# A four-layer network on one core: fp32 turns as TensorE transposes, no longer as matmuls with the identity

## The chip, the core and the metric

The kernel runs on one core of a Trainium2 chip. The core has five engines with a queue each: TensorE (PE in the profile, with its weight loads shown apart as PEld), VectorE (DVE), ScalarE (ACT), GpSimd (POOL) and SyncE (SP), which here issues all the DMA transfers. The metric is the device time of one execution in microseconds. A profile of one execution stands beside it; its span runs from the first to the last instruction.

## What is computed

An image batch x of shape (4, 96, 64, 64) in fp32 passes through four layers. Seen as tokens it is 16,384 tokens (4 images of 4,096) of 96 channels.

- Layer 0: two Mamba blocks. Each normalises every token over its 96 channels, projects, runs a short causal convolution and a selective scan along the tokens, gates and projects back; then comes a fusion with a pooled branch and a batch norm.
- Layer 1: a 7 x 7 depthwise convolution, a norm over the channels, an MLP with a Gelu, scaling and the residual.
- Layer 2: a norm, linear attention without a softmax, and an MLP in emulated fp8.
- Layer 3: a norm, a filter in Fourier space along the tokens, and another MLP in emulated fp8.

The parts that the change touches, cut from the reference:

```python
# layer 0, in each of its two blocks
mu = seq.mean(-1, keepdims=True)
var = ((seq - mu) ** 2).mean(-1, keepdims=True)
h = (seq - mu) * jax.lax.rsqrt(var + EPS) * ln_g + ln_b
...
# layer 1
h = conv_general_dilated(x, conv_w, padding=((3, 3), (3, 3)), feature_group_count=dim)
h = jnp.transpose(h + conv_b[None, :, None, None], (0, 2, 3, 1))
h = (h - mu) * jax.lax.rsqrt(var + LN_EPS) * ln_g + ln_b
h = jax.nn.gelu(jnp.einsum('bhwc,cf->bhwf', h, w1) + b1, approximate=False)
h = jnp.einsum('bhwf,fc->bhwc', h, w2) + b2
...
# layer 2
attn = jnp.einsum('bhnd,bhmd->bhnm', q, k) * D ** (-0.5)
y = jnp.einsum('bhnm,bhmd->bhnd', attn, v)
```

## The kernel before

Channels lie on the partitions (96 of them) and tokens along the free dimension nearly everywhere. In four places the kernel needs tokens on the partitions, or comes back from there, and turns tiles of 128 tokens by 96 or 97 channels. A matmul computes the transpose of its stationary operand times the moving one, so a product of a tile with the identity turns it. The result lands in PSUM and ACT or DVE copies it out.

- Layer 0, `first_stage`, slot -3 (L308). The work is cut into 32 items: 4 images by 4 chunks of 1,024 tokens by 2 blocks. Each item passes 24 scan tiles of 128 x 1,024: per tile ACT does an exponential (`da`, `dap`), PE repeats B over the partitions (`rep`, L454), DVE multiplies (L486) and scans (L490), POOL multiplies by C (L496), PE sums into `y` (L515). Beside the scans of one item run the norm and the projections of a later one, spread over time slots written by hand. In the norm `nt` holds tokens on partitions; 8 products with `ident` turn it back into `ps`, and ACT copies it into `n` (L323), which feeds the projections `w_x` and `w_z` (L210).
- Layer 1, token stage (`tokens`, `turn`, L744). For each of 16 chunks of 1,024 tokens, two loads (`o`, `xr`), an ACT scaling (L736) and a DVE addition (L737) make `t`; `turn` then turns 8 tiles into `xt_ps` in two halves of four. ACT copies the first half into `xt` (L750), DVE the second (L748).
- Layer 1, convolution: 24 groups of 4 channels, each a product of `xt` with a band matrix (1 MB a group, three buffers, L761) on PE. Ahead of group 8 `consts2` prepares the constants of all later layers: its loads, its DVE and ACT work, and three small products on PE stand in the queues at that place.
- Layer 1, norm and MLP: 32 blocks of 512 tokens. `stats` (DVE, L810, L811), `roots` (ACT), `back` (DVE makes four slices `n`, L824; PE turns them into `tp_ps`, L829; DVE copies to `xc`, L831), `hidden` (PE, L838, ACT Gelu, L839) and `out` (PE, L844, DVE adds into `t`, L847).
- Layer 2, attention: 32 blocks of 512 tokens. `scale` (`v_ps`, L894, then two ACT operations), `center` (`xc_ps`, L888, then ACT's square), `norm` (DVE, L900), `turn` (PE turns 4 tiles of 128 tokens by 97 rows into `ht_ps`, L935; ACT copies to `ht`, L939), `products` (`gram`, L947), and from a lag of 11 blocks on `out` (`o_ps`, L985). The attention runs without a softmax, so the 97 x 97 product `gram` of an image is all it needs of the turned tokens. In one step of the loop `back` comes before `out`, `center` before `products`, and `turn` before `out`.

The order of the instructions on PE, DVE, ACT and POOL is the program's own, since these four are named in the manual schedule:

```python
engines = {mybir.EngineType.PE, mybir.EngineType.DVE, mybir.EngineType.Activation, mybir.EngineType.Pool}
```

SP is not among them. The order of the DMA issues on its queue is made by a scheduler, from its own estimate of when each instruction becomes ready. A load that finds its buffer still in use, or the semaphore that it would reuse still owed by an earlier load, holds back everything behind it on SP. In `consts2` the buffers `w1raw` and `w2raw` are single, so the loads for the second fp8 MLP (`f3`) wait for the casts of the first (`f2`).

The layer 1 block loop, which sets the order around L829:

```python
hidden(i)
...
for i2 in (1, 2) if i == 0 else (i + 2,):
    if i2 < 4 * n:
        back(i2)
...
if d:
    out(i - 1)
```

Of the kernel before, what the change touches and what calls it, by code (L numbers as in the profile page):

```python
# [18 lines left out]
B, C, HW, L = 4, 96, 64, 4096  # L19
# [31 lines left out]
class Net:  # L51
# [43 lines left out]
    def layer0(self, dram, scratch):  # L95
        tc, nc, ins = self.tc, self.nc, self.ins
        x_in = ins["x"]
        with ExitStack() as ctx:
# [43 lines left out]
            n = cp.tile([C + 1, T + 3], F32, name="n")  # L142
# [56 lines left out]
            def tile_ps(rows=C):  # L199
                return psum.tile([128, MB], F32, name="ps", tag="ps")[:rows]  # L200
# [54 lines left out]
            def first_stage(k):  # L255

                b, s, i = items[k]
                m = made[k]
                steps = {}

                def at_slot(t):
                    def keep(f):
                        steps.setdefault(t - 24, []).append(f)

                    return keep

                @at_slot(-11)
                def _():
                    m["xn"] = load_x(b, s, i) if k else x0
# [34 lines left out]
                @at_slot(-3)  # L304
                def _():
                    m["ps"] = [tile_ps(), tile_ps()]
                    for q in range(8):
                        nc.tensor.matmul(  # L308
                            m["ps"][q // 4][:, q % 4 * 128 : q % 4 * 128 + 128],
                            m["nt"][:, q],  # L310
                            self.ident,
                            start=True,
                            stop=True,
                        )

                @at_slot(-2)
# [251 lines left out]
            with tc.manual_schedule(engines=engines):  # L568
                gp = global_pool()
                first = min(stages[0])  # L570
                for m in range(first, last + 19):
                    k, t = divmod(m, NTL)
# [39 lines left out]
            d = cp.tile([C, 1], F32, name="bn_d0")  # L612
# [100 lines left out]
    def layer1(self, scratch, t):  # L713
        tc, nc, ins = self.tc, self.nc, self.ins
# [3 lines left out]
        with ExitStack() as ctx:  # L718
# [4 lines left out]
            with (  # L723
                tc.manual_schedule(engines=engines),
                tc.tile_pool(name="l1a", bufs=1) as wk,
                tc.tile_pool(name="l1ap", bufs=1, space=PSUM) as psum,
            ):
                for at in (slice(0, 2), slice(NR + 2, NR + 4)):
                    nc.gpsimd.memset(xt[:, :, :, at], 0.0)
                def tokens(b, s):  # L730
                    at = slice(b * L + s * T, b * L + (s + 1) * T)
                    o = wk.tile([C, T], F32, name="o", tag="o", bufs=3)
                    nc.sync.dma_start(o, scratch[:, at])
                    xr = wk.tile([C, T], F32, name="xr", tag="xr", bufs=3)
                    nc.sync.dma_start(xr, ins["x"][b, :, s * T : (s + 1) * T])
                    nc.scalar.activation(o, o, AF.Identity, scale=self.osc, bias=self.osh)  # L736
                    nc.vector.tensor_add(t[:, at], o, xr)  # L737

                def turn(b, s):
                    for h in range(2):  # L740
                        ps = psum.tile([128, 4, 128], F32, name="xt_ps", tag="xt", bufs=4)
                        for d in range(4):
                            a = b * L + s * T + (4 * h + d) * 128
                            nc.tensor.matmul(ps[:, d], t[:, a : a + 128], self.ident[:C], start=True, stop=True)  # L744
                        r = 2 + s * (T // 128) + 4 * h
                        dst = xt[:, :, b, r : r + 4].rearrange("p c r -> p r c")
                        if h:
                            nc.vector.tensor_copy(dst, ps[:, :, :C])  # L748
                        else:
                            nc.scalar.copy(dst, ps[:, :, :C])  # L750

                chunks = [(b, s) for b in range(B) for s in range(NSC)]
                tokens(*chunks[0])
                for k, chunk in enumerate(chunks):
                    if k + 1 < len(chunks):
                        tokens(*chunks[k + 1])
                    turn(*chunk)

                def load(g):
                    w = wk.tile([128, GC, 4, 128], F32, name="band", tag="band", bufs=3)  # L760
                    nc.sync.dma_start(w, ins["band"][g])  # L761
                    return w

                def outer(g):

                    x2 = wk.tile([128, 2 * GC, B, NR], F32, name="x2", tag="x2", bufs=3)
                    at = slice(g * 2 * GC, (g + 1) * 2 * GC)
                    nc.gpsimd.tensor_copy(x2[:64], xt[:64, at, :, 4:])
                    nc.gpsimd.tensor_copy(x2[64:], xt[64:, at, :, :NR])
                    return x2  # L770

                def small(rows, cols):
                    ps = psum.tile([128, 4, 128], F32, name="w_ps", tag="xt", bufs=4)
                    return ps.rearrange("p a c -> p (a c)")[:rows, :cols]

                x2 = [outer(0)]
                for g in range(C // GC):
                    if g == 8:
                        self.consts2(wk, small)
                    if g % 2 == 0 and g + 2 < C // GC:  # L780
                        x2.append(outer(g // 2 + 1))
                    w = load(g)
                    ps = psum.tile([128, GC, B, NR], F32, name="cv_ps", tag="cv", bufs=4)
                    for d in range(GC):
                        c = g * GC + d
                        for k, j in enumerate((1, 0, 2)):
                            nc.tensor.matmul(
                                ps[:, d], w[:, d, j], xt[:, c, :, 1 + j : 1 + j + NR], start=k == 0, stop=False
                            )
                        nc.tensor.matmul(ps[:, d], w[:, d, 3], x2[g // 2][:, g % 2 * GC + d], start=False, stop=True)  # L790
                    for d in range(GC):
                        c = g * GC + d
                        dst = xt[:, c, :, 2 : 2 + NR]
                        if g % 2:
                            nc.vector.tensor_scalar_add(dst, ps[:, d], cb[:, c : c + 1])
                        else:
                            nc.scalar.activation(dst, ps[:, d], AF.Identity, bias=cb[:, c : c + 1])
# [20 lines left out]
            def back(i):  # L818
                k, d = divmod(i, 4)
                n = wk.tile([128, 4, C], F32, name="n", tag="n", bufs=3)  # L820
                for q in range(4):
                    b, r = divmod(4 * i + q, NR)
                    at = slice(4 * d + q, 4 * d + q + 1)
                    nc.vector.tensor_scalar(  # L824
                        n[:, q], xt[:, :, b, 2 + r], mv[k][:, at, 0], rs[k][:, at], ALU.subtract, ALU.mult
                    )
                ps = psum.tile([C, 4, 128], F32, name="tp_ps", tag="tp", bufs=2)
                for q in range(4):
                    nc.tensor.matmul(ps[:, q], n[:, q], self.ident, start=True, stop=True)  # L829
                xc[i] = wk.tile([C, MB], F32, name="xc", tag="xc", bufs=7)  # L830
                nc.vector.tensor_copy(xc[i], ps.rearrange("p r n -> p (r n)"))  # L831

# [17 lines left out]
            n = NT // MB // 4  # L850
# [55 lines left out]
    def layer2(self, t, h3):  # L906
        tc, nc = self.tc, self.nc
        NB = L // MB
        n = B * NB
        engines = {mybir.EngineType.PE, mybir.EngineType.DVE, mybir.EngineType.Activation, mybir.EngineType.Pool}  # L910
        with ExitStack() as ctx:
# [9 lines left out]
            for k in range(2):  # L921
                h = wk.tile([C + 1, L], F32, name=f"h{k}")
# [4 lines left out]
            def block(i):  # L927
                b, s = divmod(i, NB)
                return hs[b % 2][:, s * MB : (s + 1) * MB]

            def turn(i):
                h = block(i)
                ps = psum.tile([128, 4, C + 1], F32, name="ht_ps", tag="ht")
                for d in range(4):
                    nc.tensor.matmul(  # L935
                        ps[:, d], h[:, d * 128 : (d + 1) * 128], self.ident[: C + 1, : C + 1], start=True, stop=True
                    )
                ht[i] = wk.tile([128, 4, C + 1], F32, name="ht", tag="hts", bufs=2)
                nc.scalar.copy(ht[i], ps)  # L939

# [52 lines left out]
            for j in range(2 * n + NB + 2):  # L993
# [19 lines left out]
                if 0 <= j - 3 < n:  # L1013
                    turn(j - 3)
# [473 lines left out]
```

## Time and profile before

| | us |
|---|---|
| device time, median of 3 runs | 3931.25 |
| lowest and highest run | 3930.65, 3931.9 |
| span of the profiled execution | 3923.7 |

The stages of the profiled execution, by the window view (busy us of each engine in the stretch; the bounds are rounded, since stages overlap a little at their ends):

| stretch, us | what runs | PE | DVE | ACT | POOL | PE clock |
|---|---|---|---|---|---|---|
| 0 to 25 | first loads, first norm | 18.7 | 9.2 | 7.4 | 0.8 | 1.00 |
| 2450 to 2590 | layer 0, the last items | 94.0 | 135.8 | 65.8 | 136.3 | 0.70 |
| 2590 to 2660 | end of layer 0, layer 1's token stage | 44.7 | 35.7 | 36.0 | 4.8 | 0.85 |
| 2660 to 2790 | layer 1's convolution | 91.2 | 28.7 | 18.8 | 24.8 | 0.86 |
| 3140 to 3260 | layer 2's fp8 MLP | 108.4 | 104.4 | 97.9 | 75.8 | 1.00 |
| 3330 to 3760 | layer 3's Fourier filter | 387.1 | 212.8 | 257.3 | 196.5 | 0.98 |

The page gives PE 14,174 matmuls and 14,174 weight loads. The four lines of the turns in the trace, where each fp32 product shows as two matmuls and two loads:

| line | where | matmuls | median ns of a matmul | median ns of a load | first to last start, us |
|---|---|---|---|---|---|
| L308 | layer 0's norm | 512 | 421 | 283 | 16.7 to 2430.6 |
| L744 | layer 1's token stage | 256 | 275 | 192 | 2612.2 to 2658.6 |
| L829 | layer 1's norm | 256 | 273 | 163 | 2788.8 to 2982.1 |
| L935 | layer 2's attention | 256 | 275 | 192 | 3008.3 to 3134.7 |

How to read it: matmuls are pipelined, so that the duration of one record (from its start to its modelled end) is longer than the time for which it holds PE. That time is read from one start to the next. The PE clock is the mean that was granted in the stretch, 1.00 being full speed.

### The profile page before, as it was taken

The numbers are of one execution on the slowest core, as the hardware profiler recorded it, in microseconds if no ns is written. First come the engines' busy times: TensorE is split into PE (matmuls) and PEld (weight loads), VectorE is DVE, ScalarE is ACT, GpSimd is POOL, SyncE is SP. The second block draws the span as 40 slices with busy tenths as digits, with TensorE's granted clock in tenths as the row PEclk, the third lists the DMA queues.
The fourth block names the chain that finished last, engine by engine and source line by source line (L and its number), as shares of the span: only waits on it lengthen the run. The fifth ranks groups of instructions, "written<-read, shape, count | busy, mean of one in ns | idle before, by whom it ended". The sixth has DMA issues, their size and how long they took to land. (4 is left out here: it accounts for less than half of the span.)

```text
span 3923.7 us, 45255 instructions
## 1 busy us (share of the span) xinstructions
PE 3245.2 (83%) x14174; PEld 1384.0 (35%) x14174; DVE 3158.5 (80%) x2772; ACT 2419.1 (62%) x4644; POOL 2911.1 (74%) x1443
## 2 busy tenths in 40 slices
PE   7788878887787788888878888666899988899988
PEld 3222222222222222222222222136545634666653
DVE  5999999999999999999999999962563385444649
ACT  4666667766766676667766666541345576656558
POOL 2999999999999999999999999942001054444427
PEclk8878888888889888878897888678899999999999
DMA  7567656665666566656775666646200000011102
GB/s 188 139 158 171 151 139 166 165 161 143 162 164 163 138 167 164 163 138 165 167 162 137 166 165 163 146 125 218 73 1 1 1 1 6 14 33 36 39 7 59
DMA packets 179833, 463.39 MB, mean 118 GB/s; under 512 B 52852, under 2 KB 54782, under 8 KB 176256
## 3 DMA queue, kind: packets, MB, share of 16 engines
q1 hardware_dynamic: 179592, 460.49, 47.4%
q8 instruction: 113, 1.85, 0.2%
q14 instruction: 128, 1.05, 0.1%
HBM read 386.81 MB, written 73.50 MB: 117 GB/s over the span
## 5 line engine op out<-in xcount | busy, mean ns | idle before, releaser
L496 POOL TENSOR_TENSOR hs<-hs,crep 128x1024 f32<-128x1024 f32 x768 | 1795.5, 2361 | 28.3 <-DVE hs L490 24.5
L454 PE MATMUL rep<-dbl,sel_b 32*128 32x512 f32 x1152 | 407.2, 783 | 468.4 <-DVE hs L490 436.5
L474 POOL TENSOR_TENSOR up<-udb,brep 128x1024 f32<-128x1024 f32 x256 | 604.2, 2360 | 8.5 <-DMA brep<-cd 8.5
L468 ACT ACTIVATE da<-ddb,nega 128x1024 f32<-128x1024 f32 x512 | 585.0, 1150 | 16.0 <-DVE hs L490 9.2
L468 ACT ACTIVATE dap<-ddb,nega 128x1024 f32<-128x1024 f32 x256 | 286.2, 1118 | 422.7 <-DVE hs L490 421.2
L515 PE MATMUL y<-hs,sel_r 128*32 128x512 f32 x3072 | 480.5, 693 | 5.5 <-POOL hs L496 5.4
L490 DVE TENSOR_TENSOR_SCAN hs<-da,state,rep 128x1024 f32<-128x1024 f32 x192 | 450.8, 2348 | 16.7
L490 DVE TENSOR_TENSOR_SCAN hs<-da,state,u 128x1024 f32<-128x1024 f32 x192 | 450.9, 2348 | 11.2 <-DVE u L486 1.4
L490 DVE TENSOR_TENSOR_SCAN hs<-dap,state,up 128x1024 f32<-128x1024 f32 x192 | 447.0, 2328 | 6.0 <-ACT dap L468 5.9
L454 PEld LDWEIGHTS rep<-dbl,sel_b 32*128 32x128 f32 x1152 | 108.7, 217 | 765.9 <-issue 515.6
L210 PE MATMUL ps<-n,w_x 97*64 97x512 f32 x1536 | 364.9, 617 | 8.0 <-ACT n L323 4.4
L486 DVE TENSOR_TENSOR u<-udb,rep 128x1024 f32<-128x1024 f32 x256 | 314.7, 1229 | 44.3 <-PE rep L454 13.6
L486 DVE TENSOR_TENSOR rep<-udb,rep 128x1024 f32<-128x1024 f32 x256 | 310.6, 1213 | 0.3
L1046 POOL CAST hq<-y 128x1536 fp8e5<-128x1536 f16 x64 | 93.9, 1467 | 233.5 <-issue 137.6
L210 PEld LDWEIGHTS ps<-n,w_x 97*64 97x64 f32 x1536 | 108.9, 140 | 256.6 <-issue 212.4
L515 PEld LDWEIGHTS y<-hs,sel_r 128*32 128x32 f32 x3072 | 66.3, 116 | 354.9 <-issue 187.5
L382 POOL TENSOR_TENSOR du<-delta,xc 128x512 f32<-128x512 f32 x96 | 122.2, 1273 | 64.7 <-ACT delta L366 50.4
L918 POOL MEMSET h<- 1x4096 f32 x1 | 3.5, 3506 | 223.3 <-DVE n L824 223.3
L358 ACT COPY dbl<-ps 102x512 f32<-102x512 f32 x64 | 34.4, 589 | 199.9 <-PE ps L224 199.9
L1185 POOL TENSOR_TENSOR av<-av,ec 128x780 f32<-128x780 f32 x32 | 58.8, 1836 | 132.7 <-ACT av L1182 132.7
L224 PE MATMUL ps<-xc,xproj 64*102 64x512 f32 x384 | 154.2, 963 | 3.5 <-ACT xc L344 3.5
L490 DVE TENSOR_TENSOR_SCAN hs<-da,rep 128x1024 f32<-128x1024 f32 x64 | 146.5, 2289 | 5.4
(262 smaller groups left out, 6420.4 us busy)
## 6 DMA issues: line engine op xcount, KB each, us to landing
ddb<-dd SPq DMA_DIRECT2D x768, 128.0 KB
udb<-ud SPq DMA_DIRECT2D x768, 128.0 KB
crep<-cd SPq DMA_DIRECT2D x512, 128.0 KB
brep<-cd SPq DMA_DIRECT2D x256, 128.0 KB
dd<-delta SPq DMA_DIRECT2D x64, 384.0 KB
ud<-du SPq DMA_DIRECT2D x192, 128.0 KB
band<-in_band SPq DMA_DIRECT2D x24, 1024.0 KB
x<-in_x SPq DMA_DIRECT2D x32, 384.0 KB
```

What stands on the lines that cost most here:

```text
L210: nc.tensor.matmul(ps[rows], w[:, 64 * p : 64 * p + 64], rhs[:, at.start + shift : at.stop + shift], start=k == 0, stop=k == len(ws) - 1, ...
L224: nc.tensor.matmul(ps, w[rows, p], x[rows, p], start=start and p == 0, stop=p == 2)
L382: nc.gpsimd.tensor_mul(u, m["delta"][:, of], m["xc"][:, of])
L454: nc.tensor.matmul(x[:, at], sel_b[rows, order[t][1]], made[k]["dbl"][rows, at], start=True, stop=True)
L468: nc.scalar.activation(da, made[k]["dd", h, j], AF.Exp, scale=nega[:, col : col + 1])
L474: nc.gpsimd.tensor_mul(u, made[k]["ud", h, j], made[k]["brep", g])
L486: nc.vector.tensor_mul(u, made[k]["ud", h, j], x)
L490: nc.vector.tensor_tensor_scan(hs[:, 1:], made[k].pop(("da", t)), u, 0.0 if s == 0 else st, ALU.mult, ALU.add)
L496: nc.gpsimd.tensor_mul(hs[:, :T], hs[:, 1:], made[k]["crep", order[t][1]])
L515: nc.tensor.matmul(made[k]["y", p][row : row + 32], sel_r, made[k]["hs", t][:, at], start=False, stop=True, skip_group_check=True,)
L1046: nc.gpsimd.tensor_copy(q, y2, saturate=False)
L1185: nc.gpsimd.tensor_add(v[:, 2:4], v[:, 0:2], ec)
```

## The change

In the four places `nc.tensor.matmul(out, tile, identity, start=True, stop=True)` becomes `nc.tensor.transpose(out, tile, identity)`, which is TensorE's own transpose: a matmul instruction with its transpose flag set, with the same operands. The number of turns (640) stays. In layer 1's token stage the output and the identity are also cut from 128 to 96 columns, since a transposed tile of 96 channels has 96 columns. Tiles, buffers, copies and the order written by hand on PE, DVE, ACT and POOL stay as they are. The other products with the identity (the residual of layer 0's `project`, L533) stay matmuls.

```diff
@@ -305,12 +305,8 @@
                     m["ps"] = [tile_ps(), tile_ps()]
                     for q in range(8):
-                        nc.tensor.matmul(
-                            m["ps"][q // 4][:, q % 4 * 128 : q % 4 * 128 + 128],
-                            m["nt"][:, q],
-                            self.ident,
-                            start=True,
-                            stop=True,
+                        nc.tensor.transpose(
+                            m["ps"][q // 4][:, q % 4 * 128 : q % 4 * 128 + 128], m["nt"][:, q], self.ident
                         )
@@ -741,7 +737,7 @@
                             a = b * L + s * T + (4 * h + d) * 128
-                            nc.tensor.matmul(ps[:, d], t[:, a : a + 128], self.ident[:C], start=True, stop=True)
+                            nc.tensor.transpose(ps[:, d, :C], t[:, a : a + 128], self.ident[:C, :C])
@@ -826,7 +822,7 @@
                 for q in range(4):
-                    nc.tensor.matmul(ps[:, q], n[:, q], self.ident, start=True, stop=True)
+                    nc.tensor.transpose(ps[:, q], n[:, q], self.ident)
@@ -932,9 +928,7 @@
                 for d in range(4):
-                    nc.tensor.matmul(
-                        ps[:, d], h[:, d * 128 : (d + 1) * 128], self.ident[: C + 1, : C + 1], start=True, stop=True
-                    )
+                    nc.tensor.transpose(ps[:, d], h[:, d * 128 : (d + 1) * 128], self.ident[: C + 1, : C + 1])
```

## The prediction

> **What bounds the kernel now.** I read the page's slices first, then the busy time by stage, then the waits of the longest stage, then the order in time inside the stages where the changed instructions run.
>
> ```profile
> 25.00:2450.00 2425.00, 1966.49 (x8256) 618.02 (x8252) 2320.14 (x1327) 1608.73 (x2980) 2350.88 (x1066) 0.84 0.66 159
> ...
> 2790.00:2990.00 200.00, 191.78 (x619) 93.99 (x619) 120.90 (x409) 85.56 (x121) 3.51 (x1) 0.97 0.00 1
> ...
> 3010.00:3140.00 130.00, 126.31 (x701) 80.00 (x700) 35.10 (x54) 75.07 (x141) 0.00 (x0) 1.00 0.00 1
> ```
>
> The columns are stretch, length, then busy us of PE, PEld, DVE, ACT and POOL, PE clock, DMA share and GB/s. In layer 0 (first row) DVE and POOL are busy 96% and 97%; PE, at 81%, is not the bound. In layer 1's norm and MLP (second) and in layer 2's attention (third) PE is busy 96% and 97% and nothing else exceeds 60%. So 256 of the 640 transposes lie where PE has room, 128 (L744) in the token stage paced by loads (DMA share 1.04 in 2610 to 2650), and only the 256 of L829 and L935 where PE is the bound. What each engine waited for in layer 0, 100 to 2400 us:
>
> ```profile
> DVE u L486 <- PE rep L454: 12.3, 12, 2.9
> ...
> POOL hs L496 <- DVE hs L490: 18.8, 24, 2.4
> ```
>
> DVE waited 12.3 us for PE in 2,300 us. ACT waits 60.8 us for L308 in all (44 times), but ACT is busy only 66% and loses its time again waiting for DVE's scans. Layer 1's MLP, in order of time:
>
> ```profile
> 2852.53 2.74 PE L838 MATMUL g_ps<-xc,c_w 96*128 96x512 f32 x6
> ...
> 2855.11 1.04 PE L829 MATMUL tp_ps<-ident,n 128*96 128x128 f32 x8
> ...
> 2855.98 2.74 PE L838 MATMUL g_ps<-xc,c_w 96*128 96x512 f32 x6
> ...
> 2858.50 1.14 DVE L824 TENSOR_SCALAR n<-xt,mv,rs 128x96 f32<-128x96 f32 x4
> ...
> 2858.97 1.19 PE L829 MATMUL tp_ps<-ident,n 128*96 128x128 f32 x8 [0.25 <-DVE n L824]
> ```
>
> Four transposes hold PE from 2855.11 to the next matmul at 2855.98, 0.87 to 0.88 us: 8 matmul/load pairs (each fp32 product is two) of 110 ns. The last row is different: there PE waits for DVE's `n` slices, 0.29 us each. And layer 2:
>
> ```profile
> 3129.80 1.06 PE L935 MATMUL ht_ps<-ident,h 97*128 97x97 f32 x8
> ...
> 3130.70 1.02 PE L985 MATMUL o_ps<-h,g 97*96 97x512 f32 x2
> ...
> 3131.56 1.02 PE L894 MATMUL v_ps<-sq,ones 96*96 96x512 f32 x2
> ...
> 3132.42 1.02 PE L888 MATMUL xc_ps<-t,center 96*96 96x512 f32 x2
> ...
> 3133.28 0.85 PE L947 MATMUL gram<-ht 128*97 128x97 f32 x8
> ...
> 3133.96 1.06 PE L935 MATMUL ht_ps<-ident,h 97*128 97x97 f32 x8
> ```
>
> One block takes 4.16 us of PE without a gap; four transposes hold it for 3130.70 - 3129.80 = 0.90, some 0.86 after the overlap at the start: 107 ns a pair.
>
> [...] at L935 the matmul has 97 columns, the load 128, and the pair takes 107 ns, so the load sets the pace; at `gram` (97 and 97) it is 0.68/8 = 85. [...] no row of before shows a transpose. [...] the trace has two pairs, with 430 ns for 512 columns each.
>
> **The change, part by part.** The program built from the changed kernel has 13,534 matmuls and as many loads, against 14,174: a transpose is one pair where the product was two. My estimate of a pair: [...] 80 ns at L829 (96 columns), 107 at L935 and L744 (128). Bounds: [...] one load costing what the two did, 160 and 213 ns, no gain at L935. Dearer than the old product is the rival below.
>
> *L829, 32 groups of four.* A group goes from 0.88 to 4 x 0.08 = 0.32: 0.56 off. Counted in the timeline: 27 groups from 2821.8 on, of which 5 (2834.29, 2858.97, 2883.64, 2908.30, 2932.96) wait for `n`. In those, DVE goes from one group's end through xc (0.2 + 0.61), statistics (1.69), four `n` (1.16) to the next in about 4.0 us, which no PE speed changes: 0.1 each. For the other 22, DVE's longest round is m_ps (2.58 us after the transposes), 0.2, t 0.72, `n` 1.16, and about 0.3 to the last transpose, 5.0 us, against PE's new 2.58 + 2.58 + 0.32 = 5.48: PE stays the bound. 22 x 0.56 = 12.3, plus 0.5, plus 2 for the five early groups (two at half clock, 1.99 us of records each, about 0.85; the others partly behind `n`). Sum 14.8; bounds 6 and 17.5.
>
> *L935, 32 groups.* 0.86 becomes 4 x 0.107 = 0.43. In the last 20 blocks (4.16 us, with the o_ps product) all of it counts: 8.6. In the first 10 the block takes 3.30 us, and there a second loop lies just below: ahead of the first transposes (3000.50, 3003.51, 3006.53) v_ps comes every 3.01 us, PE waiting 1.06 us for ACT's square of the last block. So those gain 0.29: 2.9. Two blocks with the small matmuls of the weights: 0.8. Sum 12.3; bounds 0 and 16.9.
>
> *L744, 16 chunks of eight.* Loads pace the chunks (about 3 us; eight transposes take 1.75). Only the last chunk's second half stands before the convolution: 8 x 0.107 instead of 1.75, so the convolution starts about 0.9 us earlier. If that were lost again, nothing.
>
> *The SP queue, which the diff does not show.* Its DMA order is not written by hand, and with the other transposes it comes out differently in the convolution. The loads of bands 3 to 7 move up among c_w1, c_w2, ls_row, wkv, wqt and wff; the last three are now issued after band 7, between it and bn1_rows, some 0.43 us each, +1.3 us. At g = 8 PE stands still for 25 us, and this is why:
>
> ```profile
> 2681.70 3.43 SPq L680 DMA_DIRECT2D bn_rows<-in_bn_rows  x1
> ...
> 2704.11 0.45 ACT L682 ACTIVATE bn_s<-bn_rows,eps 97x192 f32<-97x192 f32 x1 [15.40 <-DMA bn_rows<-in_bn_rows]
> ...
> 2711.59 0.36 DVE L664 CAST f3w1q<-w1raw 96x384 fp8e5<-96x384 f32 x1 [16.51 <-DMA w1raw<-in_f_w]
> ```
>
> bn_rows takes 22 us to land and only then does SP issue the second w1raw and w2raw, which take 7.4 us more beside a band of 1 MB. In the new order w1raw goes earlier, w2raw still waits for bn_rows, and band 9 moves behind both (the first being 0). So: -0.9 from the early start, +1.3 from the three loads, -0.36 for a cast done ahead. I take zero for the token stage and convolution together; -5 if w2raw lands before the bands, +4 if band 9 is late.
>
> *L308, layer 0.* 8 of some 75 us of work per item; hidden under DVE and POOL in steady state. In the first item PE does L308 from 16.66 to 19.4 at half clock and the convolution could start when DVE has w_x, at 18.70: 0.65 us, and the same kind of time once more before the scans run full: 1.5 in all. Bounds +3 (PE, less busy, gets a lower clock than its 0.84, and `rep` comes later) and -4.
>
> Sum: 14.8 + 12.3 + 1.5 + 0 = 28.6 us off the span of 3923.7: 3895.1. The time outside the span (3931.25 - 3923.7 = 7.5 us) stays, so 3902.6, taken as 3903.
>
> **Rivals.** *All at a quarter:* [...] 17.5 + 16.9 + 1.5 = 36 off, 3895; with the kind ends of layer 0 and the loads 3887. [...] against: in the trace loads follow columns only. *One load as dear as two:* 6 + 0 + 1.5 off, 3924, up to 3929 with the unkind ends.[...] *Slower:* [...] Place: the same 22 and 32 groups. 4 x 0.275 = 1.10 instead of 0.88 and 0.86: 22 x 0.22 + 32 x 0.24 + 0.5 = +13, 3944. It decides from 215 ns a transpose on. [...] against: 275 ns is also what the trace records for a plain 128-column matmul here (273 median at L829), pipelined at 110, so it looks like latency.
>
> **How the numbers follow.** Forecast 0.58, all at a quarter 0.16, one dear load 0.12, slower 0.14. 0.2% is 7.9 us, about what a measurement of this kernel tells from no change, so faster means below 3923.4: 0.58 + 0.16 + half of 0.12 = 0.80; same the other half and a little, 0.07; slower 0.13. The range runs over the first three cases with their ends, 3887 to 3929, and leaves the slower case out.
>
> **What would show it.** L829's groups should hold PE 0.3 to 0.45 us, L935's 0.43, with matmul counts 512, 256, 256, 256 halved. Layer 2's block should be 3.7 us, and 3.0 early on with PE waiting for `sq`. The gated groups of layer 1 should keep their 4.0 us. PE's halt at g = 8 should end within some us of 2716. A time above 3931 with pairs over 0.2 us means the slower rival; a clock under 0.97 in these two stages would be a cause I have not priced.

## The result, and the profile after

Before and after were run together, eight times each.

| | before | after |
|---|---|---|
| median, us | 3931.97 | 3919.55 |
| lowest and highest, us | 3930.65 to 3936.74 | 3900.96 to 3925.66 |
| ratio of the times, with its 95% interval | | 0.9961 (0.9947 to 0.9976) |

The change gains 12.4 us where 28.6 were forecast. The runs of after spread over 24.7 us, those of before over 6.1. The profiled execution of after is its slowest run: span 3923.9 us, no shorter than the 3923.7 of before. So the two profiles side by side show gains and losses of equal size. Read from the starts and ends of the same instructions in both:

| stretch | before, us | after, us | difference |
|---|---|---|---|
| layer 0, first scan to end of last scan | 2515.0 | 2535.2 | +20.2 |
| first turn of the token stage to first turn of L829 (L825 after): token stage, convolution | 176.6 | 180.2 | +3.6 |
| layer 1's norm and MLP, first turn to last `m_ps` | 209.0 | 198.0 | -11.0 |
| layer 2's attention, first `xc_ps` to last `ht_ps` | 136.3 | 121.4 | -14.9 |
| from there to the end | 788.7 | 790.7 | +2.0 |

The remaining +0.3 us lies in the joints between these stretches. Since the edit is shorter than what it replaces, the same lines have smaller numbers in after: L829 is L825 there, L935 is L931, L454 is L450 and L486 is L482. Layer 1's MLP in the timeline of after (start, duration, engine, line, operation; x4 means that four instructions are merged into the row):

```profile
2868.51 0.60 PE L825 MATMUL tp_ps<-ident,n 128*96 128x128 f32 x4
2868.95 5.31 PE L840 MATMUL m_ps<-g,c_w 128*96 128x512 f32 x12
...
2876.67 0.60 PE L825 MATMUL tp_ps<-ident,n 128*96 128x128 f32 x4
2877.11 2.74 PE L834 MATMUL g_ps<-xc,c_w 96*128 96x512 f32 x6
```

Four transposes are now four instructions instead of eight, and hold PE from 2876.67 to 2877.11: 0.44 us, 110 ns each. Before it was 0.88. Layer 2's attention, in the timeline of after:

```profile
3118.31 0.50 PE L931 MATMUL ht_ps<-ident,h 97*128 97x97 f32 x4
3118.64 1.02 PE L979 MATMUL o_ps<-h,g 97*96 97x512 f32 x2
3119.50 1.02 PE L890 MATMUL v_ps<-sq,ones 96*96 96x512 f32 x2
3120.37 1.02 PE L884 MATMUL xc_ps<-t,center 96*96 96x512 f32 x2
3121.22 0.85 PE L941 MATMUL gram<-ht 128*97 128x97 f32 x8
3121.91 0.50 PE L931 MATMUL ht_ps<-ident,h 97*128 97x97 f32 x4
```

The turns hold PE for 0.33 us (3118.31 to 3118.64), 83 ns each, and the block goes round in 3.60 us instead of 4.16. So the two stages where PE is the bound gained 25.9 us together, near the 27.1 that were forecast. The loss is in layer 0. What its DVE waited for from 100 to 2400 us, in the wait view of after (engine, tile, line, releaser: us in total, times, longest):

```profile
DVE u L482 <- PE rep L450: 43.4, 36, 2.9
DVE hs L486 <- ACT dap L464: 1.8, 4, 0.6
```

DVE, the bound of this stage together with POOL, waits 43.4 us for `rep` from PE, where it was 12.3, although PE has less to do. Its clock tells why. The window view of after at one of the places where the projections `w_x` follow the turns (stretch, length, busy us of PE, PEld, DVE, ACT, POOL, then PE clock, DMA share, GB/s):

```profile
1097.80:1101.90 4.10, 0.06 (x4) 0.00 (x0) 3.94 (x3) 2.40 (x6) 4.10 (x3) 0.80 0.85 229
1101.90:1111.00 9.10, 9.05 (x24) 2.40 (x28) 8.79 (x5) 2.36 (x4) 9.10 (x5) 0.53 1.02 228
```

The same view of before, at the like place of the same item:

```profile
1095.60:1098.10 2.50, 0.10 (x4) 0.03 (x1) 2.36 (x3) 2.47 (x9) 2.50 (x3) 1.00 1.04 270
1098.10:1107.90 9.80, 9.29 (x44) 2.60 (x45) 9.50 (x6) 3.47 (x8) 9.18 (x4) 1.00 1.05 232
```

After the turns PE stands idle for 4.1 us in after, 2.5 in before; then it works at a granted clock of 0.53 in after, of 1.00 in before. PE's timeline of after at that place, with idle time and its releaser in brackets:

```profile
1095.79 1.08 PE L308 MATMUL ps<-ident,nt 128*96 128x128 f32 x8
1096.80 1.06 PE L511 MATMUL y<-hs,sel_r 128*32 128x512 f32 x8
1101.95 2.08 PE L450 MATMUL rep<-dbl,sel_b 32*128 32x512 f32 x4 [4.09 <-DVE u L482]
1103.96 6.89 PE L210 MATMUL ps<-n,w_x 97*64 97x512 f32 x16
1110.79 1.06 PE L511 MATMUL y<-hs,sel_r 128*32 128x512 f32 x8
1111.78 3.66 PE L210 MATMUL ps<-n,w_x 97*64 97x512 f32 x16
1115.37 1.13 PE L450 MATMUL rep<-dbl,sel_b 32*128 32x512 f32 x4
```

And that of before:

```profile
1092.66 2.04 PE L308 MATMUL ps<-ident,nt 128*96 128x128 f32 x16 [0.68 <-ACT nt L302]
1094.63 1.06 PE L515 MATMUL y<-hs,sel_r 128*32 128x512 f32 x8
1098.10 1.13 PE L454 MATMUL rep<-dbl,sel_b 32*128 32x512 f32 x4 [2.41 <-DVE u L486]
1099.16 3.65 PE L210 MATMUL ps<-n,w_x 97*64 97x512 f32 x16
1102.75 1.06 PE L515 MATMUL y<-hs,sel_r 128*32 128x512 f32 x8
1103.74 3.65 PE L210 MATMUL ps<-n,w_x 97*64 97x512 f32 x16
1107.90 1.13 PE L454 MATMUL rep<-dbl,sel_b 32*128 32x512 f32 x4 [0.51 <-DVE hs L490]
```

The turns took 1.0 us instead of 2.0. Then the first 16 matmuls of `w_x` take 6.89 us in place of 3.65. From one `rep` to the next it is 1115.37 - 1101.95 = 13.4 us instead of 9.8. In before PE had 0.51 us to spare ahead of the second `rep`; in after it has none, and DVE waits (its timeline):

```profile
1116.54 1.23 DVE L482 TENSOR_TENSOR u<-udb,rep 128x1024 f32<-128x1024 f32 x1 [2.69 <-PE rep L450]
```

This comes back: from the first scan of one item to that of the next, before mostly takes 78.4 to 78.6 us in its steady state, while after goes round in a cycle of four items, 78.1 to 78.5, 79.1 to 79.5, 81.3 and 78.6. The place shown is the worst of the four. From the first start of the first 16 matmuls of `w_x` to the last, the mean clock from 1000 us on is 0.60, 0.50, 1.00 and 0.64 in turn in after, cycle for cycle, and 1.00 in every item of before.

The traces of before and after hold records of the granted clock, 258 and 260 of them. Each is 0.5 or 1.0, and each but the last of a trace lasts a multiple of 3.413 us. Cut into steps of this length at the bounds of the records, with PE's busy share of each step worked out from the starts of its instructions (an instruction holds PE until its end or the next start, whichever comes first), the place above reads:

```
before   step from     1090.2  1093.6  1097.0  1100.5  1103.9  1107.3
         busy share      0.80    0.61    0.69    1.00    1.00    0.85
         clock           1.0     1.0     1.0     1.0     1.0     1.0
after    step from     1090.0  1093.5  1096.9  1100.3  1103.7  1107.1  1110.5
         busy share      0.45    0.63    0.29    0.51    1.00    1.00    1.00
         clock           1.0     1.0     1.0     0.5     0.5     0.5     1.0
```

After the step with 0.29 the clock falls, and here PE fills two whole steps before it is back. By then the projections are nearly done. In the traces of before and after together the clock rose 257 times, each time after a step at least 0.84 busy, and fell 259 times, never after a step over 0.69.

Four items of the cycle take 317.4 us in after; four items of before, at 78.48 us, take 313.9. Why it is a cycle of four was not shown.

### The profile page after: what moved, and what is told of

Same layout as the page of the kernel before. It is cut to its first block, busy times and chain, and to the rows that moved or that the text cites. A ratio compares the mean times of both kernels' runs of the same rounds, so it can differ in the third digit from the quotient of the medians.

```text
span 3923.9 us, 43975 instructions
## 1 busy us (share of the span) xinstructions
PE 3205.9 (82%) x13534; PEld 1294.8 (33%) x13534; DVE 3154.4 (80%) x2772; ACT 2420.6 (62%) x4644; POOL 2911.4 (74%) x1443
## 5 line engine op out<-in xcount | busy, mean ns | idle before, releaser
L450 PE MATMUL rep<-dbl,sel_b 32*128 32x512 f32 x1152 | 407.8, 785 | 495.8 <-DVE hs L486 428.3
L486 DVE TENSOR_TENSOR_SCAN hs<-da,state,rep 128x1024 f32<-128x1024 f32 x192 | 450.8, 2348 | 16.7
L486 DVE TENSOR_TENSOR_SCAN hs<-da,state,u 128x1024 f32<-128x1024 f32 x192 | 450.9, 2348 | 11.2 <-DVE u L482 1.4
L486 DVE TENSOR_TENSOR_SCAN hs<-dap,state,up 128x1024 f32<-128x1024 f32 x192 | 446.7, 2326 | 0.4 <-ACT dap L464 0.4
L210 PE MATMUL ps<-n,w_x 97*64 97x512 f32 x1536 | 408.0, 679 | 9.3 <-ACT n L319 6.6
L482 DVE TENSOR_TENSOR u<-udb,rep 128x1024 f32<-128x1024 f32 x256 | 314.7, 1229 | 74.4 <-PE rep L450 46.0
L450 PEld LDWEIGHTS rep<-dbl,sel_b 32*128 32x128 f32 x1152 | 107.0, 214 | 794.5 <-issue 595.7
L482 DVE TENSOR_TENSOR rep<-udb,rep 128x1024 f32<-128x1024 f32 x256 | 310.3, 1212 | 0.2
L210 PEld LDWEIGHTS ps<-n,w_x 97*64 97x64 f32 x1536 | 118.6, 153 | 295.2 <-issue 243.5
L486 DVE TENSOR_TENSOR_SCAN hs<-da,rep 128x1024 f32<-128x1024 f32 x64 | 146.5, 2289 | 5.4
L486 DVE TENSOR_TENSOR_SCAN hs<-da,u 128x1024 f32<-128x1024 f32 x64 | 146.4, 2288 | 3.7 <-DVE u L482 0.5
```

The source lines that it names most:

```text
L210: nc.tensor.matmul(ps[rows], w[:, 64 * p : 64 * p + 64], rhs[:, at.start + shift : at.stop + shift], start=k == 0, stop=k == len(ws) - 1, ...
L450: nc.tensor.matmul(x[:, at], sel_b[rows, order[t][1]], made[k]["dbl"][rows, at], start=True, stop=True)
L482: nc.vector.tensor_mul(u, made[k]["ud", h, j], x)
L486: nc.vector.tensor_tensor_scan(hs[:, 1:], made[k].pop(("da", t)), u, 0.0 if s == 0 else st, ALU.mult, ALU.add)
```

## The experiments

Each kernel was timed in five rounds beside the kernel before (e4_fill has four times on record, e7_delay six). Those of layer 0 and its turns alone or undone (e1 to e4) ran together, with before at 3932.12 us; e5 to e8 together, with before at 3930.91; e9 and e10 together, with before at 3930.31. Each group ran on another chip. Between these groups the ratios are compared, not the times.

**Only layer 0's turns undone: e1_rest.** The diff is against after.

```diff
-                        nc.tensor.transpose(
-                            m["ps"][q // 4][:, q % 4 * 128 : q % 4 * 128 + 128], m["nt"][:, q], self.ident
+                        nc.tensor.matmul(
+                            m["ps"][q // 4][:, q % 4 * 128 : q % 4 * 128 + 128],
+                            m["nt"][:, q],
+                            self.ident,
+                            start=True,
+                            stop=True,
                         )
```

> The turns of layer 1 and of the attention stay transposes, layer 0's norm goes back to the matmul with the identity. Theory (the loss sits in layer 0: shorter turns there leave PE's clock low when the projections start, so that rep comes late for DVE): layer 0 goes back to about 2515 us from the first scan to the end of the last, DVE's waits for rep to about 12 us, and the median to 3902 to 3908 with a spread of a few us. Rival (the loss is not bound to these eight transposes but to the whole program's timing, or to the chip of that run): layer 0 stays near 2535 us, the median near 3920, with a spread of some 25 us.

Measured: 3903.12 us, ratio 0.9924 (0.9910 to 0.9938). Layer 0 takes 2514.9 us again, and DVE's wait reads:

```profile
DVE u L486 <- PE rep L454: 15.8, 17, 3.0
```

**Only layer 0's turns changed: e2_l0only**, the reverse: before, with the L308 block of after.

> Only layer 0's norm uses the transpose. Theory: layer 0 alone becomes 5 to 25 us longer, so the median is 3937 to 3957, slower than before, with the wide spread of the changed kernel. Rival: the turns of layer 0 are hidden either way, and the median is within 0.2% of before.

Measured: 3951.53 us, ratio 1.0042 (1.0028 to 1.0055), slower than before. Layer 0 takes 2534.6 us.

```profile
DVE u L482 <- PE rep L450: 45.0, 42, 2.8
```

The two parts nearly add up: -29.0 and +19.4 us make -9.6, against -12.4 for the whole change. Three of the four edits gain what the whole was forecast to; the fourth, priced at -1.5, gives more than half of it back.

**Each turn of layer 0 done twice: e3_twice.** The diff is against after. The second round writes the same values to the same place.

```diff
-                    for q in range(8):
+                    for q in range(16):
+                        q %= 8
                         nc.tensor.transpose(
```

> The changed kernel, with each of layer 0's eight transposes done twice, so that they hold PE as long as the eight fp32 products did (16 pairs). Theory A (the clock follows how long PE is busy, with whatever): layer 0 goes back to about 2515 us and the median to 3902 to 3908, although PE has more to do. Theory B (work in transpose mode does not count for the clock): the clock after the turns stays low, layer 0 stays at 2530 us or more, the median at 3918 or more.

Measured: 3902.11 us, ratio 0.9924 (0.9911 to 0.9936), layer 0 2513.3 us.

```profile
DVE u L483 <- PE rep L451: 11.8, 12, 2.8
```

More work on PE than in after, and layer 0 is 21.9 us shorter. What was lost is not a price of the transpose as such. It comes from the work that PE no longer does.

**Four plain fp32 products ahead of the eight transposes: e4_fill.** Again against after; the transposes overwrite the results.

```diff
+                    for q in range(4):
+                        nc.tensor.matmul(
+                            m["ps"][q // 4][:, q % 4 * 128 : q % 4 * 128 + 128],
+                            m["nt"][:, q],
+                            self.ident,
+                            start=True,
+                            stop=True,
+                        )
                     for q in range(8):
                         nc.tensor.transpose(
```

> The changed kernel, with four fp32 products ahead of layer 0's eight transposes, written to the same PSUM and overwritten by them: 8 product pairs and 8 transpose pairs, the same 16 pairs as before the change. Theory A (how long PE is busy): layer 0 about 2515 us, median 3902 to 3908. Theory B (transposes don't count): half of the old counted work, so a layer 0 between, 2515 to 2535 us. If the lost time has nothing to do with the clock, the added 0.9 us of PE work per item leaves layer 0 at 2535 us or makes it longer.

Measured: 3897.89 us, ratio 0.9915 (0.9902 to 0.9929), layer 0 2516.3 us, 15.3 us of waits for `rep`. With products as filling layer 0 comes back to 2516.3 us, with transposes to 2513.3.

**How much filling it takes: e9_half and e10_thrice.** As e3_twice, with `range(12)` and `range(24)`.

> All turns as transposes, four of L308's eight done twice (12 in place of 8 in the changed kernel and 16 in the run with each done twice). Theory (the work that PE does ahead of the projections decides its clock there): in part back, layer 0 between 2516 and 2530 us, median between 3904 and 3916, waits of u for rep between 15 and 40 us. Rival (there is one sharp limit, or the doubled work matters only by something that comes with all eight): at one of the two ends, 2513 to 2516 or 2531 to 2536.

> All turns as transposes, L308's eight done three times each (24). Theory (once the clock is up, more work ahead of the projections brings nothing more and, being off the path of VectorE, costs little): layer 0 2512 to 2517 us, median 3899 to 3905. Rival (more work goes on lifting the clock and takes away the last 12 us of waits for rep): layer 0 2503 to 2511, median 3889 to 3898. Second rival (the longer turns are late themselves): layer 0 2520 or more.

Measured with 12: 3903.65 us, ratio 0.9933 (0.9920 to 0.9945), layer 0 2516.4 us, 13.7 us of waits for `rep`: all of the loss is back with half of the doubling. Layer 0 lies at the edge of both ranges (the theory's began at 2516, the rival's ended there), but the waits and the median lie outside the theory's. So the expectation of a partial recovery failed, and what came is one of the rival's two ends: layer 0 lies 20.2 us above before with 8 turns and 1.4 with 12. With 24: 3895.83 us, 0.9917 (0.9903 to 0.9930), layer 0 2512.0 us and 10.1 us of waits, as the theory said for layer 0; the median lies in the rival's range, but the interval of its ratio and that of e3_twice overlap for the most part. PE's timeline of e9_half shows how the clock returns:

```profile
1168.18 2.08 PE L451 MATMUL rep<-dbl,sel_b 32*128 32x512 f32 x4 [4.17 <-DVE hs L487]
1170.19 2.79 PE L309 MATMUL ps<-ident,nt 128*96 128x128 f32 x12
1172.91 1.89 PE L512 MATMUL y<-hs,sel_r 128*32 128x512 f32 x8
1175.40 1.13 PE L451 MATMUL rep<-dbl,sel_b 32*128 32x512 f32 x4 [0.61 <-DVE u L483]
1176.46 3.66 PE L210 MATMUL ps<-n,w_x 97*64 97x512 f32 x16
```

and after, at the like place of an earlier item, how it does not:

```profile
1015.29 2.08 PE L450 MATMUL rep<-dbl,sel_b 32*128 32x512 f32 x4 [4.16 <-DVE hs L486]
1017.30 1.94 PE L308 MATMUL ps<-ident,nt 128*96 128x128 f32 x8
1019.17 1.94 PE L511 MATMUL y<-hs,sel_r 128*32 128x512 f32 x8
1022.51 2.07 PE L450 MATMUL rep<-dbl,sel_b 32*128 32x512 f32 x4 [1.41 <-DVE u L482]
1024.52 5.67 PE L210 MATMUL ps<-n,w_x 97*64 97x512 f32 x16
```

Both start at half clock (the first `rep` takes 2.08 us), after 4.2 us of idling. With 12 transposes PE works without a gap from 1168.18 to 1174.80, 6.6 us; by the window view the clock is 0.53 from 1168 to 1175 and 1.00 from 1175 to 1185. With 8 PE works from 1015.29 to 1021.11, 5.8 us, and then stands idle 1.41 us ahead of the second `rep`. The steps of 3.413 us from 1015.0 on are 0.90, 0.80, 0.78 and 1.00 busy, and by the clock's records full clock comes only at 1028.6. The `rep` (2.07 us against 1.13) and most of `w_x` (5.67 against 3.66) run slowly.

**A later start of the projections, with no more work on PE: e7_delay.** Against after; ACT's copies are done twice.

```diff
                     for at, ps in zip(halves, m["ps"]):
                         nc.scalar.copy(n[:C, 3 + at.start : 3 + at.stop], ps)
+                        nc.scalar.copy(n[:C, 3 + at.start : 3 + at.stop], ps)
```

> The changed kernel, with ScalarE's copies of ps into n done twice each, so that the projections start about 1.2 us later after the turns, with no more work on PE. Theory (layer 0 loses because PE is busy too little for its clock): layer 0 stays at 2530 us or more and the median at 3915 or more. Rival (what matters is only that the projections follow the turns too early, in a spell that PE's clock is still low): layer 0 back to about 2515 us, median about 3903.

Measured: 3920.55 us, ratio 0.9969 (0.9956 to 0.9981), layer 0 2533.7 us: the theory's numbers. But the run did not do what it was made for. In its timeline `w_x` starts 8.17 us after the turns (1103.34 - 1095.17), the same 8.17 as in after (1103.96 - 1095.79), because `w_x` stands behind a `rep` that waits for DVE, not for ACT's copies. It shows only that ACT's copies play no part. So a later start alone stays untested. What speaks against the rival is the timelines themselves: in before `w_x` follows 6.50 us after the turns, earlier than in after, and at full clock.

**The token stage: e5_mlp_attn, e6_fill_token, e8_token_twice.** With layer 0 mended, the stretch from the first turn to the convolution took 53.4 us in e1_rest against 47.6 in before, with PE at half clock. Three runs ask whether L744's transposes cost this. The first two take L744 back to matmuls (in e1_rest and in e4_fill):

```diff
-                            nc.tensor.transpose(ps[:, d, :C], t[:, a : a + 128], self.ident[:C, :C])
+                            nc.tensor.matmul(ps[:, d], t[:, a : a + 128], self.ident[:C], start=True, stop=True)
```

The third is e1_rest with each of L744's transposes done twice:

```diff
-                        for d in range(4):
+                        for d in (0, 0, 1, 1, 2, 2, 3, 3):
```

> Turns of layer 0's norm (L308) and of the token stage (L744) are matmuls again, those of layer 1's MLP and of layer 2's attention stay transposes. Theory (PE's shorter turns in the token stage leave PE at half clock there, and that costs the first convolution 2 to 6 us): the token stage reaches the convolution in about 47.6 us as before, layer 0 takes about 2515 us, and the median is 3897 to 3901. Rival (L744's transposes are free, as predicted): no better than the run with L308 alone undone, about 3903.

> L308 transposes with four extra fp32 products ahead of them, L744 as matmuls, the other two as transposes. Theory: both gains add, layer 0 about 2516 us and the token stage as before, median 3893 to 3898. Rival (L744 does not matter): the same as with L744 as transposes, 3898 or more.

> The kernel with L308 alone undone, with each of L744's transposes done twice. Theory (clock): PE is at full clock again in the token stage, the convolution starts about 47.6 us after the stage begins, and the time is 2 to 5 us under that with L308 alone undone (3903.1). Rival (the order of SP's queue, or something else that L744 moves): it starts after 50 to 53 us as there and the time stays at 3903.

Measured: e5_mlp_attn 3906.93 us, 0.9934 (0.9920 to 0.9947); e6_fill_token 3900.08, 0.9924 (0.9912 to 0.9937); e8_token_twice 3908.98, 0.9944 (0.9931 to 0.9956). None beats its counterpart: the theory falls. The window view of the stage in before:

```profile
2615.00:2650.00 35.00, 26.76 (x197) 24.66 (x196) 23.14 (x25) 23.85 (x25) 0.00 (x0) 0.94 1.04 271
```

In e5_mlp_attn:

```profile
2615.00:2650.00 35.00, 26.69 (x173) 25.06 (x172) 21.46 (x22) 20.63 (x21) 0.00 (x0) 0.83 1.04 239
```

In e1_rest:

```profile
2615.00:2650.00 35.00, 15.99 (x84) 13.06 (x85) 20.60 (x22) 19.57 (x21) 0.00 (x0) 0.50 1.04 234
```

In e10_thrice:

```profile
2615.00:2650.00 35.00, 18.06 (x95) 14.54 (x94) 22.45 (x24) 23.02 (x24) 0.00 (x0) 0.50 1.04 263
```

The DMA share, second from the right, is 1.04 in all four, while the last column differs: 271, 239, 234 and 263 GB/s. From the first turn to the convolution it takes 47.6, 51.6, 53.4 and 47.8 us. e10_thrice has transposes and half clock and is as fast as before; e5_mlp_attn has matmuls and 0.83 and is slow. The slowest of all, 54.4 us, is e2_l0only, which leaves L744 as it was. In the four rows the time goes with the rate of the transfers, not with the edit or the clock, and this rate differs from one profile to the next (234 to 271 GB/s); why it does was not tried. So the +3.6 us of after in this stretch (256 GB/s in its 35 us from 2635 on) needs no cost of L744. e8_token_twice did not lift the clock either: by the window view PE is busy for 30.82 of the 35 us from 2615 on, and the clock stays at 0.50. So it says nothing of what a full clock there would bring; the four rows above do.

**What beats both kernels.** e1_rest, e3_twice, e4_fill, e6_fill_token, e9_half and e10_thrice, at 0.9915 to 0.9933, cannot be told apart, since their intervals overlap. The simplest is e1_rest: transposes everywhere but in layer 0.

## Why the prediction was right, and where it was not

*Sign and range.* 3919.55 lies in the range of 3887 to 3929, and the sign is the one called likeliest, but the gain is less than half of the forecast. The two terms for the stages where PE is the bound add up nearly as forecast; the one for layer 0 is wrong in sign and size. That the median still falls into the range is luck in part: the range reached up to 3929 for a transpose as dear as 160 and 213 ns, and 110 and 83 came. (The 3929 itself counts only layer 0's unkind end; with the +4 of the convolution beside it the sum is 3932.)

*L829.* Forecast -14.8, measured -11.0. A group went from 0.88 to 0.44 instead of 0.32: the estimate of a transpose at 80 ns (as much as the 107 ns of L935's pair by the columns of the load, 107 x 96/128) should have been 110. Twenty-two groups at 0.44 are 9.7. The groups that wait for `n` gave 0.14 each, as said (a group's period 6.17 became 6.03). The early groups brought less than the 2 us set for them: about 0.6 is left for these after 9.7 and 0.7.

*L935.* Forecast -12.3, measured -14.9. A group went from 0.89 to 0.33 instead of 0.43. (The forecast had taken 0.86 for the 0.90 that it read off, so its 107 ns a pair was 111.) The early blocks went from 3.30 to 3.02 us, the floor that was forecast at 3.01. The later 20 blocks gained 0.56 each, 11.2 instead of 8.6.

*Which of the two sets the pace*, matmul or load, was the mis-sized term behind both. The forecast took the load for the longer of the two and left its time as it was: at L935 107 ns a pair, before and after. That this holds for a transpose was the author's estimate. The profiles show the reverse: a transpose holds PE 110 ns for 128 moving columns and 83 ns for 97, 0.86 ns a column, the pace of one fp32 matmul before (430 ns for 512 columns, 0.84). There is one where there were two, and it did not get faster. The load of 128 columns fits into 83 ns, where a pair of the product took 111, so it shrank; the records of a load went from 192 to 141 ns. The errors cancel: 25.9 measured for both stages, 27.1 forecast.

*L744, the SP queue and the convolution.* Forecast 0 (-5 to +4). The profile has +3.6, which the lower rate of the transfers can explain without the edit. PE's halt ahead of the constants, in its wait view, was 24.9 us before and is 24.2 in after, as little changed as was said. That SP holds loads back shows in its wait view of before from 2600 to 2785 us: 69.6 us in 18 waits at L761 for PE (`cv_ps`), 7.3 us at L662 for `bn_rows` to land. Here "loads pace the chunks" held.

*L308* is the step that failed. It said: "hidden under DVE and POOL in steady state", -1.5, with a bound of "+3 (PE, less busy, gets a lower clock than its 0.84, and `rep` comes later)". The mechanism named in the bracket is the one that came, at 20 us in the profiles, which show the slowest executions, and at 19.4 us in the medians of the single edit (by its ratio, 0.42%, some 17). The mean clock of layer 0, 0.82 in after and 0.84 in before by the window view, hides it: what counts is the clock over the projections that follow the turns. In three of the four items of the cycle it fell, in the 9 us of the place shown to 0.53 instead of 1.00. The forecast priced the turns by what they cost and not by what they keep going.

*The rivals.* "All at a quarter" (3895) and "one load as dear as two" (3924) fall by the 110 and 83 ns: a quarter of a product's 220 ns would be 55, two loads 160 and 213. Nothing in the profile of before showed why a turn should cost a quarter. The median lies near the 3924 of the second, for another reason. The slower rival, every transpose served alone for the 275 ns of its record, needed 215 ns and falls too: the record of a transpose at L829 still lasts 273 ns while it holds PE for 110, so such a figure is a latency, as the forecast guessed. What would have made the change slower is L308 alone, as e2_l0only shows.

## What to carry to other kernels

Work on PE can keep PE's clock high even where PE is not the bound: here eight transposes more an item took 21.9 us off layer 0. Before taking such work away, read the granted clock just after it (here 0.53 against 1.00) and how long PE stands idle around it (4.1 us against 2.5). Replace fp32 turns by transposes where PE is the bound (here four turns hold PE 0.44 us instead of 0.88, and 0.33 instead of 0.89), and leave or pad them where PE idles between short bursts (here e1_rest and e3_twice, both at 0.9924 against the 0.9961 of after). A pair of profiles that shows no difference in span may hold two differences of over 20 us, so compare stage by stage.

## What the runs showed of the hardware

- Transposes lifted the clock here, as products did. In e3_twice, at 1090.12 us in its timeline, `rep` takes 2.08 us after 4.16 us of idling; 16 transposes follow and hold PE 3.6 us; the next `rep`, at 1097.35, takes 1.13. With 8 transposes at such a place (after, 1015.29) the next `rep` still takes 2.07. DVE's waits for `rep` are 43.4 us in after, 11.8 in e3_twice with transposes added and 15.3 in e4_fill with products added. A clock that stays low under transposes is seen too: in the token stage of e8_token_twice it is 0.50 over 35 us in which PE is busy 88%.
- The busy share as worked out here does not settle the clock alone. In the traces of before and after, of the steps of 3.413 us at half clock, 94 of the 118 that were 0.80 to 0.98 busy were followed by half clock again, and so were 96 of the 329 over 0.98. Of the steps at full clock, 38 of the 243 that were 0.60 to 0.75 busy were followed by half clock, and 28 of the 128 of 0.30 to 0.50 were not. In 2615 to 2650 us before has 76% and a clock of 0.94, e8_token_twice 88% and 0.50. What else plays a part is open.
- The wide spread of after, 24.7 us over eight runs, is not explained. e2_l0only and e7_delay, which also have the bare eight transposes at L308, spread over 14.4 and 12.9 us, but so do e5_mlp_attn, which has matmuls there (13.2), and before itself in one of the groups (12.6). The fastest execution of after took 3900.96 us; whether its layer 0 went round in the cycle of four is not known, since no profile of it was taken.
